# Heads of an attention block on one core: TensorE keeps the written order, both halves of an output-weight block run together behind a context, and one query moves from the start to the thirteenth head

## The chip, the cores and the metric

The kernel runs on one core of one Trainium2 chip. The core has a matrix engine (TensorE, "PE" in the profile, with its weight loads listed apart as "PEld"), a vector engine (VectorE, DVE), a scalar engine (ScalarE, ACT), a general engine (GpSimd, POOL) and a sync engine (SP) that here only issues DMAs. Each engine takes its own instructions strictly in the order in which they stand in its queue; an instruction whose operands or buffers are not ready makes everything behind it in that queue wait. The metric is the device time of one execution in microseconds (us), the median of several runs.

## The reference

Two transformer layers on `x` of shape (4, 512, 1024) in float32: four batches of 512 positions, 1024 wide.

```python
x = x + L0_attn(layernorm(x))   # attention over the batch axis, at each position of the width
x = x + L0_ffn(layernorm(x))    # 1024 -> 1024, and 2 of 8 low-rank experts per token
x = x + L1_attn(layernorm(x))   # below
x = x + L1_ffn(layernorm(x))    # 1024 -> 1024, and 8 low-rank experts weighted per batch
```

The change lies wholly in the third line, whose attention has 32 heads of width 128 (64 without and 64 with rotary position) and a shared latent of 64 for keys and values:

```python
q = rmsnorm(x @ wq_a.T) @ wq_b.T              # 1024 -> 256 -> 32 heads x (64 + 64)
ckv, k_pe = split(x @ wkv_a.T)                # 64 + 64, the same for all heads
kv = rmsnorm(ckv) @ wkv_b.T                   # 64 -> 32 heads x (64 key + 128 value)
q_pe, k_pe = rope(q_pe), rope(k_pe)
scores = einsum('bqhd,bkhd->bhqk', q, k) * scale     # causal mask, softmax
out = einsum('bhqk,bkhd->bqhd', softmax(scores), v)  # 512 x (32 x 128)
return out @ wo.T                                    # 4096 -> 1024
```

## The kernel before

Everything is one program, `block_kernel`. Products need close to float32 accuracy, so most operands are split into a rounded high part (type fp32r, names ending in `h`) and the remainder (`l`), and a product is three matmuls: `matmul3` (L148) does low x high, high x low, high x high in one PSUM bank.

The stages in order of time: layer 0 and the query, key and value projections of layer 1 (to 421.7 us), the *heads* (421.7 to 1488.3 us), and the last feed-forward. The change touches the heads alone.

**Units.** The 32 heads are four groups of eight (`NG`, `HG`); for each group come the four batches, and in each batch the eight heads: `units` is a list of 128 triples (g, b, i). One iteration of the loop over `u` works on several units at once, at different stages:

- `split_query(u + 1)` (L737): DVE makes the rounded copy `qh` (L741) and POOL the remainder `ql` (L742) of the next unit's query.
- `scores(u)`: four row tiles of 512, 384, 256 and 128 columns, one after another in a pool `pss` of two PSUM banks. The first three are `matmul3`, the last is one float32 matmul (L913). Each is followed by a DVE instruction that adds the causal mask and takes the minimum (L919) and by ACT's exponential (L922).
- `turn(u - 1)`: ten transposes of the previous unit's probabilities (L943) in three lots into a pool `pst` of two banks; the lots are copied to `pT` by ACT, ACT and DVE (L945).
- `context(u - 3)` on odd `u`, for two units at a time: eight matmuls 64 columns wide into `psv` (L959), and a DVE multiplication by the divisors (L962). The divisors go through a DRAM round trip on SP (`r_d`, `rb`).
- `query(u + 3)` (six matmuls into the single bank `psq`) and `rotate_query(u + 3)`: ACT copies it to `qf` (L729), DVE makes two half products from the bank (`wA`, L731 and L732), POOL multiplies and adds (L733, L734). Unit 2's query is issued in iteration 0, unit 3's likewise, and so on, three units ahead.
- a *filler*, a generator that is advanced by `per[0]`, `per[1]` and `per[2]` steps at three places of the iteration: behind the 384-column scores and the context, behind the 128-column scores and two lots of transposes, and behind the query.

**Two kinds of filler.** `project(g, b)` multiplies a finished batch's context by the group's output weights, in the seven-product form of Strassen and Winograd, twice (`j` = 0 and 2): products b11, t1, t2, b22, t3, b21, t4, each of two halves (so a filler step is half a product: "t40" is the first half of t4), accumulate in two banks `poa` and `pob`. After a product DVE adds the bank into a tile `xs` (L1036) that was fetched from DRAM and goes back there. The left operands `cxh` and `cxl` are made by ACT (L993) and POOL (L994). `prepare_output(g)` makes the group's output weights (value weights times `wo`): `block(n, half, at)` issues two matmuls 64 columns wide (L1069) into `poa` or `pob` from a room (`slotC`) that `fetch_output` fills by DMA (L1047, L1049); four blocks of two halves a group. ACT keeps a copy of a bank in one of six pieces of a room `raw` (`kept`, L1078) or makes a high part (`high`, L1083); the low parts and the differences between pieces (`low`, `less`) go to POOL when both operands are in `raw` (L1089, L1096), and to DVE when one is a bank (L1092, L1099). The names of the weights' tiles are those of the products: `b110h` is the high part of the first b11 tile, `t31h` that of the second t3 tile. For group 0 these steps run in the iterations u = 3 to 10, beside no projection; for groups 1 to 3 in four iterations at a time (u = 39 to 42 and so on), where the first batch of a group ends.

`prepare_query` (L677) makes a half group's query weights in the bank `pob`, from DRAM by `fetch_query`, in the iterations (b, i) = (3, 3) and (0, 0).

**What sets the order.** In the heads the framework's scheduler decides each engine's order from the written program, its own estimates and priorities, and `tc.issue_after(...)`, which holds an instruction behind a named one. On PE it moves work considerably: transposes, halves of a query and halves of products are found elsewhere than written. The last feed-forward already has `tc.manual_schedule(...)`, which makes the named engines take their instructions in the order of the program text.

## Time and profile before

| | us |
|---|---|
| median of 3 runs (lowest to highest) | 1746.12 (1744.06 to 1748.56) |
| the profiled execution | 1748.5 |
| its span, first to last instruction | 1746.3 |

The granted clock of TensorE is 0.997 of full speed over the span. Three stages of the span:

| stage | length, us | PE busy | DVE busy | ACT busy | POOL busy |
|---|---|---|---|---|---|
| before the heads, 0 to 421.67 | 421.67 | 401.39 | 316.29 | 170.06 | 127.64 |
| heads, 421.67 to 1488.30 | 1066.63 | 1056.85 | 802.24 | 631.01 | 651.43 |
| behind the heads, to 1746 | 257.70 | 246.40 | 187.10 | 102.43 | 146.21 |

How to read it. "Busy" is the time in which an instruction of the engine ran; an engine that waits for an operand is not busy. The span leaves out 2.2 us of the profiled execution's time, around the first and last instruction. A row of a timeline has the start in us, the duration, the engine, the line and the operation, the tile written and the tiles read, the shape, and in square brackets the idle time ahead of it and what ended that. A row of windows has the stretch, its length, the busy time and number of instructions of PE, PEld, DVE, ACT and POOL, the granted clock, the share of time in which the DMA engines were busy and the GB/s they moved.

### The profile page before, as it was taken

The page shows a single profiled execution, that of the slowest core. Times are in us where ns is not written, and L with a number is a line of the kernel's source. Part 1 is how long each engine was busy: PE and PEld are TensorE (multiplying, and loading weights), DVE is VectorE, ACT ScalarE, POOL GpSimd, SP SyncE. Part 2 cuts the span into 40 slices and gives each one's busy share as a digit, 9 for nine tenths or more (in the row PEclk, how much of TensorE's full clock was granted, in tenths as well). Part 3 has the DMA queues.
Part 4 walks back from the last instruction along what each step waited for, and adds up shares of the span by engine and source line. Part 5 has one row for each costly group of instructions (what it writes and reads, how often), then busy time and mean ns, then how long its engine had stood idle before and what let it go on. Part 6 is the DMA issues. An engine that isn't in the chain of part 4 may idle for free.

```text
span 1746.3 us, 31729 instructions
## 1 busy us (share of the span) xinstructions
PE 1704.6 (98%) x10536; PEld 1432.1 (82%) x10536; DVE 1305.6 (75%) x3494; ACT 903.5 (52%) x2316; POOL 925.3 (53%) x926
## 2 busy tenths in 40 slices
PE   7999999999999999999999999999999999999999
PEld 6899999998767777767787767778777877789998
DVE  7977885676877777787777677777778777687675
ACT  7422331365765565475555476555466555453332
POOL 0553541202666565666666656666556664675454
PEclk9999999999999999999999999999999999999999
DMA  5313543245324234353333353242344333853431
GB/s 194 134 42 116 183 161 114 89 137 166 103 92 140 97 108 148 98 175 113 113 126 105 113 183 116 97 148 94 130 159 156 108 101 121 308 199 123 138 110 68
DMA packets 131940, 228.17 MB, mean 131 GB/s; under 512 B 22272, under 2 KB 58752, under 8 KB 128448
## 3 DMA queue, kind: packets, MB, share of 16 engines
q1 hardware_dynamic: 131776, 226.13, 38.7%
q8 instruction: 84, 1.38, 0.3%
q14 instruction: 80, 0.66, 0.1%
HBM read 156.60 MB, written 71.83 MB: 131 GB/s over the span
## 4 chain that ended last, share of the span: by engine, by line
PE 85%; DVE 7%; DMA 3%; ACT 2%; POOL 2%; issue 2%; SPq 0%; DVEq 0%; ACTq 0%; POOLq 0%
PE psv L959 8%; PE pst L943 8%; PE pss L150 4%; PE po L150 4%; PE po L152 4%; PE po L151 4%; PE pss L151 4%; PE pss L152 4%; PE pob L150 3%; PE psq L150 3%; PE poa L150 3%; PE psq L151 3%; PE psq L152 3%; PE pob L152 3%; PE pob L151 3%; PE acc L150 3%
## 5 line engine op out<-in xcount | busy, mean ns | idle before, releaser
L922 ACT ACTIVATE p<-p,mn 128x512 f32<-128x512 f32 (+3 forms) x512 | 284.6, 558 | 218.6 <-DVE mn L919 214.3
L919 DVE CUSTOM_DVE_ANT_0 p<-pss,causal 128x512 f32<-128x512 f32 (+3 forms) x512 | 232.4, 486 | 29.1 <-PE pss L152 21.9
L733 POOL TENSOR_TENSOR qf<-qf,ropeT 64x512 f32<-64x512 f32 x128 | 164.5, 1285 | 167.1 <-ACT qf L729 165.1
L943 PE MATMUL pst<-ident,p 128*128 128x128 f32 x1280 | 186.1, 273 | 3.7 <-ACT pT L945 3.7
L734 POOL TENSOR_TENSOR qf<-qf,wA 64x512 f32<-64x512 f32 x128 | 164.5, 1285 | 31.2 <-DVE wA L732 24.8
L943 PEld LDWEIGHTS pst<-ident,p 128*128 128x128 f32 x1280 | 153.0, 141 | 31.1 <-ACT pT L945 8.2
L742 POOL TENSOR_TENSOR ql<-qf,qh 128x384 fp32r<-128x384 f32 x128 | 131.1, 1024 | 63.9 <-DVE qh L741 47.6
L994 POOL TENSOR_TENSOR cxl<-s,cxh 128x256 fp32r<-128x256 f32 x128 | 96.8, 764 | 119.0 <-ACT cxh L993 65.1
L945 ACT COPY pT<-pst 128x512 f32<-128x512 f32 x256 | 142.4, 578 | 23.3 <-PE pst L943 21.3
L150 PE MATMUL pss<-kT,ql 128*128 128x512 f32 (+2 forms) x384 | 144.0, 375 | 0.8 <-DVE mn L919 0.4
L150 PE MATMUL po<-w_h,hTl 128*128 128x384 f32 (+1 forms) x384 | 133.1, 347 | 0.8 <-DVE x L433 0.8
L151 PE MATMUL pss<-kT,qh 128*128 128x512 f32 (+2 forms) x384 | 131.5, 342 | 0.0
L152 PE MATMUL pss<-kT,qh 128*128 128x512 f32 (+2 forms) x384 | 130.4, 340 | 0.0
L152 PE MATMUL po<-w_h,hTh 128*128 128x384 f32 (+1 forms) x384 | 130.1, 339 | 0.0
L151 PE MATMUL po<-w_l,hTh 128*128 128x384 f32 (+1 forms) x384 | 129.7, 338 | 0.0
L945 DVE COPY pT<-pst 128x256 f32<-128x256 f32 x128 | 54.3, 424 | 94.2 <-PE pst L943 93.1
L729 ACT COPY qf<-psq 128x512 f32<-128x512 f32 x126 | 74.0, 587 | 71.7 <-PE psq L152 71.7
L731 DVE TENSOR_TENSOR wA<-psq,ropeT 32x512 f32<-32x512 f32 x126 | 87.7, 696 | 22.5 <-ACT qf L729 19.5
L994 POOL TENSOR_TENSOR cxl<-cx,cxh 128x256 fp32r<-128x256 f32 x96 | 73.7, 769 | 55.6 <-ACT cxh L993 53.1
L922 ACT ACTIVATION_READ_ACCUMULATOR p<-p,mn 128x1 f32 x512 | 96.9, 189 | 0.0
L150 PEld LDWEIGHTS pss<-kT,ql 128*128 128x128 f32 x384 | 72.6, 189 | 21.9 <-DVE mn L919 4.3
L732 DVE TENSOR_TENSOR wA<-psq,ropeT 32x512 f32<-32x512 f32 x126 | 87.0, 691 | 1.7
(511 smaller groups left out, 4979.1 us busy)
## 6 DMA issues: line engine op xcount, KB each, us to landing
xs<-x_d SPq DMA_DIRECT2D x128, 256.0 KB
x_d<-xs SPq DMA_DIRECT2D x128, 256.0 KB
slotC<-in_woT_dram SPq DMA_DIRECT2D x32, 512.0 KB
rb<-r_d SPq DMA_DIRECT2D x128, 128.0 KB
w_t<-raw SPq DMA_DIRECT2D x32, 288.0 KB
x<-in_x_dram SPq DMA_DIRECT2D x16, 512.0 KB
x_d<-x SPq DMA_DIRECT2D x32, 256.0 KB
slotA<-q_d SPq DMA_DIRECT2D x8, 1024.0 KB
```

The costliest lines, as they stand in the source:

```text
L150: T.matmul(ps, lhsT=al, rhs=bh, start=start, stop=False, **kw)
L151: T.matmul(ps, lhsT=ah, rhs=bl, start=False, stop=False, **kw)
L152: T.matmul(ps, lhsT=ah, rhs=bh, start=False, stop=stop, **kw)
L733: G.tensor_tensor(f[mid], f[mid], ropeT[mid, 0, :], ALU.mult)
L734: G.tensor_tensor(f[mid], f[mid], t2[mid], ALU.add)
L742: G.tensor_tensor(l, f[:, P:S], f32(h), ALU.subtract)
L919: turn_of[0] = V.tensor_tensor_reduce(out=to, in0=ps[:, 0:n], in1=causal[:, S - n : S], scale=1.0, scalar=-NEG, op0=ALU.add, op1=ALU.min, ...
L922: A.activation(to, to, AF.Exp, bias=mn[:, i : i + 1], scale=-1.0, accum_out=rs[:, i : i + 1])
L943: T.transpose(ps[:, w : w + P], p[:, OF[i] + j * P : OF[i] + (j + 1) * P], ident)
L945: copy(pT[:, AT[js[0]] : AT[js[0]] + w], ps[:, 0:w])
L959: T.matmul(ps[n * KVR : (n + 1) * KVR, S - w : S], lhsT=k[:, j, :], rhs=pTs[u + n][:, AT[j] : AT[j] + w], start=(j == 0), stop=(j == TPB - 1))
L994: G.tensor_tensor(l, src, f32(h), ALU.subtract)
```

## The change

It has six parts, all in the heads:

1. `manual_schedule` for TensorE: its instructions of the heads stay in the order of the program text. The other engines are still ordered by the scheduler.
2. Queries come two units ahead instead of three up to u = 12 (`EXTRA`), and three ahead afterwards; iteration 12 issues two of them (units 14 and 15), so one query moves from the start to the thirteenth head. Up to u = 12 `split_query(u + 1)` stands behind the first advance of the filler.
3. A block of the output weights does both halves, in `poa` and `pob`, in one step, behind a context. Four of these steps a group replace eight; `per` for group 0 becomes (1, 1, 1), and for heads 4 to 7 of a group's first batch (2, 2, 2).
4. The differences and low parts of the output weights are taken in another order and with other pieces: more of them are between pieces of `raw`, which puts them on POOL, and there are fewer copies on ACT. Group 0 has an order of its own.
5. `less` looks only at its two operands to choose the engine, so a difference can be written from a bank into `raw`.
6. `prepare_query` moves from the iteration into `project`, ahead of each half (`j` = 0 and 2), into the bank whose turn it is; a list `fetched_q` holds what was fetched.

```diff
--- before.py
+++ after.py
@@ -849,6 +849,7 @@
         xsp = c2.enter_context(tc.tile_pool(name="c2_x", bufs=5, side="right"))
         pso = c2.enter_context(tc.tile_pool(name="c2_pso", bufs=1, space=PSUM, side="right"))
         heads = c2.enter_context(ExitStack())
+        heads.enter_context(tc.manual_schedule(engines={T.engine}))
         tp = heads.enter_context(tc.tile_pool(name="c2_t", bufs=3))
 
 
@@ -1014,6 +1015,9 @@
                             splitter(cxp, HG // 4, "cx"))
             parts = [next(outs), next(outs)]
             for j in range(0, TPB, 2):
+                if fetched_q:
+                    n, fetched = fetched_q.pop(0)
+                    wqs[n] = prepare_query(fetched, pso, "po" + "ab"[(1 + j // 2) % 2])
                 at, xs, banks = {}, {}, {}
                 for t, k in ((0, 0), (1, 1), (0, 1), (1, 0)):
                     at[t, k] = x_d[b * TPB + j + t][k]
@@ -1060,15 +1064,16 @@
             prs = [c + k for c in range(HG // 4) for k in (0, HG // 4)]
             po, tiles = {}, {}
 
-            def block(n, half, at):
+            def block(n):
                 nonlocal fetched
                 wo, wv = fetched
-                po[at] = pso.tile([P, 512], F32, name="po" + at)
                 with ExitStack() if g else tc.issue_after(scored[0].ins):
-                    for k in range(2):
-                        T.matmul(po[at][k * KVR : (k + 1) * KVR, :], lhsT=wv[:, k, :],
-                                 rhs=wo[k][:, half * 512 : half * 512 + 512], start=True, stop=True)
-                if half and n + 1 < len(prs):
+                    for half, at in enumerate("ab"):
+                        po[at] = pso.tile([P, 512], F32, name="po" + at)
+                        for k in range(2):
+                            T.matmul(po[at][k * KVR : (k + 1) * KVR, :], lhsT=wv[:, k, :],
+                                     rhs=wo[k][:, half * 512 : half * 512 + 512], start=True, stop=True)
+                if n + 1 < len(prs):
                     fetched = fetch_output(g, prs[n + 1])
 
             def src(at):
@@ -1092,89 +1097,66 @@
                     V.tensor_tensor(l, src(at), f32(h), ALU.subtract)
 
             def less(to, a0, a1):
-                if not {to, a0, a1} & set(po):
+                if not {a0, a1} & set(po):
                     G.tensor_tensor(src(to), src(a0), src(a1), ALU.subtract)
                     return
                 with tc.issue_after(turn_of[0].ins):
                     V.tensor_tensor(src(to), src(a0), src(a1), ALU.subtract)
 
             def steps():
-                block(0, 0, "a")
-                yield
-                kept(0, "a")
-                high("b11", "a")
-                block(0, 1, "b")
-                yield
-                low("b11", "a")
-                kept(1, "b")
-                yield
-                less("b", "b", 0)
-                block(1, 0, "a")
...
+                for n in (0, 2):
+                    block(n)
+                    yield
+                    kept(1, "b")
+                    yield
+                    high("b11", "a")
+                    less(4, 1, "a")
+                    yield
+                    low("b11", "a")
+                    yield
+                    high("t1", 4)
+                    yield
+                    low("t1", 4)
+                    yield
+                    block(n + 1)
+                    yield
+                    if g == 0:
+                        kept(3, "b")
+                        less(5, "b", 4)
+                        high("b21", "a")
+                        yield
+                        kept(2, "a")
+                        high("b22", 3)
+                        low("b21", "a")
+                        yield
+                        high("t2", 5)
+                        low("b22", 3)
+                        less(3, 3, 1)
+                        low("t2", 5)
+                        yield
+                        high("t3", 3)
+                        less(2, 2, 5)
+                        low("t3", 3)
+                        yield
+                    else:
+                        less(5, "b", 4)
+                        high("b22", "b")
+                        yield
+                        low("b22", "b")
+                        less(2, "a", 5)
+                        high("b21", "a")
+                        yield
+                        less(3, "b", 1)
+                        low("b21", "a")
+                        high("t2", 5)
+                        yield
+                        low("t2", 5)
+                        high("t3", 3)
+                        low("t3", 3)
+                        yield
+                    high("t4", 2)
+                    low("t4", 2)
+                    yield
 
             return steps()
 
@@ -1211,7 +1193,9 @@
                     nc.sync.dma_start(out=tiles[t][:, k * 512 : (k + 1) * 512], in_=x_d[2 * q + t][k])
 
         filler = None
+        fetched_q = []
         cx = None
+        EXTRA = 12
         for u in range(NU + 3):
 
 
@@ -1219,12 +1203,12 @@
             g, b = divmod(B, NB)
             if i == 0 and B > 0:
                 filler = project(*divmod(B - 1, NB))
-            per = ((4, 1, 0) if i % 2 else (1, 1, 0)) if b else (2 + (i < HG // 2 + 2), 2, 2) if i >= HG // 2 else (3, 3, 1)
+            per = ((4, 1, 0) if i % 2 else (1, 1, 0)) if b else (2, 2, 2) if i >= HG // 2 else (3, 3, 1)
             if B == 0:
-                per = (0, 1, 2)
+                per = (1, 1, 1)
             if b == 0 and i == (HG // 2 if g else 0) and g < NG:
                 filler = prepare_output(g, wo_raw)
-            if u + 1 < NU:
+            if EXTRA < u < NU - 1:
                 split_query(u + 1)
             sc = scores(u) if u < NU else iter(())
             tn = turn(u - 1) if 0 < u <= NU else iter(())
@@ -1234,10 +1218,11 @@
             advance(sc)
             advance(cx)
             advance(filler, per[0])
+            if u <= EXTRA:
+                split_query(u + 1)
 
             if u == 0:
                 query(2, psq, "psq")
-                rotate_query(2)
             advance(sc)
             advance(sc)
             advance(tn)
@@ -1245,15 +1230,18 @@
             advance(filler, per[1])
             if u < NU:
                 g, b, i = units[u]
-                if (b, i) == (NB - 1, 3) and g + 1 < NG:
-                    wqs[2 * g + 2] = prepare_query(wq_raw, pso, "pob")
-                if (b, i) == (0, 0) and g > 0:
-                    wqs[2 * g + 1] = prepare_query(wq_raw, pso, "pob")
-            if u + 3 < NU:
+            if 0 < u <= EXTRA:
+                query(u + 2, psq, "psq")
+            if u <= EXTRA:
+                rotate_query(u + 2)
+            if EXTRA < u < NU - 3:
                 query(u + 3, psq, "psq")
                 rotate_query(u + 3)
             advance(filler, per[2])
             advance(tn)
+            if u == EXTRA:
+                query(u + 3, psq, "psq")
+                rotate_query(u + 3)
             if u < NU:
                 g, b, i = units[u]
                 if i == 2 and u + HG < NU:
@@ -1262,7 +1250,8 @@
                 if b == 0 and i == 0:
                     wo_raw = fetch_output(g, 0)
                 if (b, i) in ((NB - 1, 0), (NB - 1, 4)) and g + 1 < NG:
-                    wq_raw = fetch_query(2 * g + 2 + i // 4)
+                    n = 2 * g + 2 + i // 4
+                    fetched_q.append((n, fetch_query(n)))
                 if (g, b) == (NG - 1, NB - 1) and i == 1:
                     late = raw()
                     hs = {0: [late[:, (t + 1) * D : (t + 2) * D] for t in range(2)]}
```

More of the change, by code (lines that the diff above doesn't have):

```diff
@@ L1101, in steps @@
             def steps():
-                block(0, 0, "a")
-                yield
-                kept(0, "a")
-                high("b11", "a")
-                block(0, 1, "b")
-                yield
-                low("b11", "a")
-                kept(1, "b")
-                yield
-                less("b", "b", 0)
-                block(1, 0, "a")
-                yield
-                high("t1", "b")
-                kept(0, "b")
-                kept(2, "a")
-                high("b21", "a")
@@ L1118, in steps @@
-                yield
-                low("t1", "b")
-                low("b21", "a")
-                block(1, 1, "b")
-                yield
-                high("b22", "b")
-                kept(3, "b")
-                yield
-                low("b22", 3)
-                less("b", "b", 0)
-                block(2, 0, "a")
-                yield
-                high("t2", "b")
-                kept(5, "a")
-                less(3, 3, 1)
-                yield
-                low("t2", "b")
@@ L1135, in steps @@
-                less("b", 2, "b")
-                high("b11", "a")
-                yield
-                high("t4", "b")
-                high("t3", 3)
-                low("b11", "a")
-                yield
-                low("t4", "b")
-                low("t3", 3)
-                block(2, 1, "a")
-                yield
-                kept(1, "a")
-                yield
-                less("a", "a", 5)
-                block(3, 0, "b")
-                yield
-                high("t1", "a")
@@ L1152, in steps @@
-                kept(5, "a")
-                kept(2, "b")
-                high("b21", "b")
-                yield
-                low("t1", "a")
-                low("b21", "b")
-                block(3, 1, "a")
-                yield
-                high("b22", "a")
-                kept(3, "a")
-                yield
-                low("b22", 3)
-                less("a", "a", 5)
-                yield
-                high("t2", "a")
-                less(3, 3, 1)
-                yield
@@ L1169, in steps @@
-                low("t2", "a")
-                less("a", 2, "a")
-                high("t3", 3)
-                yield
-                high("t4", "a")
-                low("t3", 3)
-                yield
-                low("t4", "a")
-                yield
+                for n in (0, 2):
[51 more added lines that the diff above has]
+                    yield
```

## Prediction

> **What bounds the kernel now.** I read the page's engine table first, then the stages by window, then the order of instructions on TensorE (PE) against its helpers.

> ```profile
> PE 1704.6 (98%) x10536; PEld 1432.1 (82%) x10536; DVE 1305.6 (75%) x3494; ACT 903.5 (52%) x2316; POOL 925.3 (53%) x926
> ```

> PE is the bound. Only its waits and the form of its order can change the time: the change adds and removes no matmul. The heads run from 421.7 to 1488 us. By windows (length, then busy us of PE, PEld, DVE, ACT, POOL, then the granted clock):

> ```profile
> 426.00:430.00 4.00, 1.32 (x6) 0.85 (x5) 2.30 (x5) 0.75 (x2) 3.24 (x4) 1.00 0.96 281
> 430.00:436.00 6.00, 5.62 (x18) 4.19 (x18) 3.22 (x12) 3.52 (x11) 2.61 (x3) 0.50 0.32 104
> 442.00:515.00 73.00, 70.75 (x402) 50.09 (x401) 58.42 (x162) 52.75 (x142) 47.63 (x42) 1.00 0.34 116
> 515.00:676.00 161.00, 161.00 (x911) 126.66 (x910) 119.55 (x325) 91.62 (x256) 100.35 (x98) 1.00 0.34 112
> 742.00:800.00 58.00, 57.20 (x317) 39.19 (x314) 46.99 (x124) 42.00 (x108) 37.74 (x35) 1.00 0.47 152
> ```

> The first two are the start (2.7 us idle, then half clock), 442 to 515 is heads 3 to 13, 515 to 676 heads with projection and not one idle PE moment, 742 to 800 the output weights of group 1. So nearly every microsecond by which PE waits anew is lost. An even-numbered u with projection, from the timeline:

> ```profile
> 622.33 0.39 PE L152 MATMUL psq<-slotB,wqh 128*128 128x512 f32 x1
> ...
> 622.76 0.59 ACT L729 COPY qf<-psq 128x512 f32<-128x512 f32 x1 [0.57 <-PE psq L152]
> ...
> 623.42 0.70 DVE L731 TENSOR_TENSOR wA<-psq,ropeT 32x512 f32<-32x512 f32 x1
> ...
> 624.85 0.69 DVE L919 CUSTOM_DVE_ANT_0 p<-pss,causal 128x512 f32<-128x512 f32 x1
> ...
> 625.46 0.55 DVE L919 CUSTOM_DVE_ANT_0 p<-pss,causal 128x384 f32<-128x384 f32 x1
> ...
> 625.85 0.40 PE L152 MATMUL poa<-b211h,cxh 128*128 128x512 f32 x1
> ...
> 625.94 0.68 DVE L1036 TENSOR_TENSOR xs<-xs,pob 128x512 f32<-128x512 f32 x1
> ...
> 626.08 0.28 PE L150 MATMUL pss<-kT,ql 128*128 128x256 f32 x1
> ...
> 626.77 0.47 PE L150 MATMUL pob<-t40h,cxl 128*128 128x512 f32 x1
> ```

> The query's last matmul gives way at 622.56; call such a moment Q. Behind it stand, in DVE's order, the rotation (L731, L732) from Q+0.86, the masks of 512 and 384 columns from Q+2.29 and Q+2.90, and the sum L1036, which ends at 626.62. Product t40 accumulates in the bank that the sum reads and starts 0.15 us after its end. PE fills the time with the 256-column and 128-column scores.

> **The change, step by step.** The built order of the changed kernel gives what stands where. Sums go against the profiled execution: 1748.5 us with a span of 1746.3, 2.4 above the median of the runs, 1746.1.

> *1. t40 in the projection.* PE's order as written puts t40's first half directly behind b21, ahead of the 256-column scores; DVE's order there is unchanged. PE is ready at 626.08 and may start at 626.77: 0.69 us of waiting, and the scores queued behind have no cover left to give. In before the same place loses 0.10 (626.55 to 626.77 instead of 0.11), so 0.58 net. The timeline shows the pattern 19 times (530.08, 562.33, 594.54, 626.77, 659.91, five and five again, four in the last group). Of the other five, three (690, 961, 1232) escape because the query was put later; as written it is not: 0.69 each. The last two have no query before them. 19 x 0.58 + 3 x 0.69 = **+13.1**. Ends: 0, if the sum gets done earlier, and 22 x 0.69 = 15.2.

> *2. Even heads without projection (u = 2, 4, 8).* In before the scheduler put eight transposes and half a query between the 384- and the 256-column scores (440.64 to 442.48). As written nothing is between: PE arrives at Q + 0.22 (two transposes) + 0.70 + 0.53 = Q+1.45. The 256-column scores need the buffer that the 512-column mask frees at Q+2.98, plus 0.15: Q+3.13, and the 128-column ones the 384 mask, Q+3.45 plus 0.15. Waiting 1.65 + 0.14 = 1.8 each: **+5.4**. Odd heads have context (2.3) and block in that place and wait for nothing. Ends 0 and 6.

> *3. u = 6 and 10 (seventh and eleventh head).* In before a chain of GpSimd (POOL) work of the output weights stops PE once:

> ```profile
> 491.61 1.28 POOL L1096 TENSOR_TENSOR raw<-raw 128x512 f32<-128x512 f32 x1
> ...
> 492.92 0.62 ACT L1083 CAST t31h<-raw 128x512 fp32r<-128x512 f32 x1 [2.48 <-POOL raw L1096]
> ...
> 493.45 0.72 ACT L922 ACTIVATE p<-p,mn 128x512 f32<-128x512 f32 x1
> ...
> 495.64 1.05 ACT L945 COPY pT<-pst 128x512 f32<-128x512 f32 x2
> ...
> 496.26 0.44 PE L943 MATMUL pst<-ident,p 128*128 128x128 f32 x2 [2.25 <-ACT pT L945]
> ```

> ScalarE (ACT) waits for POOL, its exponentials and copies of transposes queue behind, and PE's third group of transposes lacks a buffer. The change puts ten subtractions into POOL's queue for group 0 plus four, where six were, and queries come two heads ahead, not three. For u = 6 POOL's order is: b220l, two subtractions, first rotation of query 7, t20l, t30l, second rotation, t40l, ql. From Q of u = 4: the second block ends at 1.45 + 2.4 + 1.9 = 5.75; four ACT copies at 0.5 to 0.6 each bring b220h at 7.7; seven POOL pieces (five subtractions, two rotations) at 1.35 bring 17.2. DVE then makes qh (0.3), which stands ahead of the 256-column mask in its queue, and the mask (0.4); ACT two exponentials (0.9) and a copy (0.5): PE's transposes go on at 19.5. Without waits PE is there after an odd head (1.45 + 2.4 + 1.9 + 0.58 + 0.87 + 1.39 = 8.6) and an even one's 4.3, at 12.9. 6.6 lost. u = 10 has the same pieces in another order; I take the same. 2 x 6.6 - 2.25 (the old stop) = **+11.0**. Ends 2.25 and 8 for each head.

> *4. The additional query (u = 12).* In before query 3 runs at 429.05, inside idle time at the start, 6 x 0.23 = 1.4 us. The start's chain (masks from 430.58, behind a DMA) stays, so the early slot is not made use of, and 1.4 is paid between full heads. Its bank is single and query 14 is just before it: like the 2.68 us gap at 426.4, PE waits for the rotation, Q+2.4 plus 0.15 against Q+0.22: 2.3. **+3.7**, ends 0 and 4.1.

> *5. Blocks.* Blocks and contexts are 64 columns wide.

> ```profile
> 485.43 0.39 PE L152 MATMUL psq<-slotB,wqh 128*128 128x512 f32 x1
> 485.75 1.08 PE L1069 MATMUL poa<-slotC 128*64 128x512 f32 x4
> 486.76 0.44 PE L943 MATMUL pst<-ident,p 128*128 128x128 f32 x2
> ```

> Entry costs 0.32 here where a product gives way after 0.23, and the exit 0.10 more: 0.19 a round trip. By the order, 87 runs of 64-wide instructions become 70: 17 x 0.19 = **-3.2**. The waits of the output-weight stretches (0.49 and 0.31 three times, 0.61 at 1293) go: **-3.0**. In groups 1 to 3 two blocks are now one head apart: 4.3 us of PE work lie between, while a fetch takes from 745.25 to about 749.7 in the packets, with wake-up 4.7. 0.4 x 6 = **+2.4**, ends 0 and 7 (behind the 1 MB load of the next batch).

> *6. SP and the rest.* Four fetches a group as before; query weights come as many heads ahead. The ACT copies saved (0.5 us each) lie beside PE: nothing.

> *7. The clock.* 2.7 us idle, after gaps of 0.56 and 0.48, was followed by 6 us at 0.50, which lost 3; 2.25 us idle at 494 kept 1.00. The new gaps, about 2 and 4 us, stand amid work; I take 0, end +6. [...]

> Sum: 13.1 + 5.4 + 11.0 + 3.7 - 3.2 - 3.0 + 2.4 = **+29.4**: 1777.9 against the profiled execution, 1775.5, say **1776**, on the median's scale.

> **Rivals.** *A: the GpSimd chain costs only what it cost before* (2.25 a head, so -8.7): 1767. For it: ACT and POOL are each under 75% busy there. Against: POOL takes turns strictly in the rows above.
> *B: no wait at t40* (-13.1): 1762. It needs DVE's sum 0.7 us earlier; but the 19 rows agree to 0.02 us.
> *C: two clock drops as at 430* (+6): 1782.
> *D, the other side: the order as written has no hazards*, because DVE gets to the masks early. From the 39th to the 44th head before needs 50.4 us for 48.0 of PE work, three times 2.4; the first twelve take 82.2 for 77.2. Saved 7.2 + 5.0: 1734. It decides from a mask start at Q+1.3 or sooner on and needs POOL clear of item 3; the rows have Q+2.29.
> *E: the order hardly differs where it counts*: 1746. For it: heads with projection are the same but for t40.

> **Numbers.** Forecast 0.45, A 0.13, B 0.12, C 0.10, D 0.14, E 0.06. 0.3% is 5.2 us, about what can be told from no change: faster 0.14, same 0.06, slower 0.80. The range 1757 to 1790 holds all but D and E: its low end is B with A's half, its high end the forecast with C, 8 us heads and slow fetches.

> **What would show it.** Right: PE idle before pob/poa of t40 by about 0.6 at some 22 places; PE idle over 5 us in each of the seventh and eleventh heads, ended by ACT's pT; 1.7 us before the 256-column scores in heads 3, 5 and 9; 2.3 before the second query of head 13. Wrong: 161 us windows in the middle still at 100% PE, or head 13 reached by 516 us instead of about 530.

## The result and the profile after

The changed kernel takes 1786.1 us (median of 4 runs, 1784.3 to 1789.3; before, on the same chip, 1745.8), 1.0228 times the time before, interval 1.0212 to 1.0243: slower by some 40 us. The forecast was 1776 in a range of 1757 to 1790. The profiled execution took 1785.8 with a span of 1783.9. Its engine table has for TensorE (PE):

```profile
PE 1700.8 (95%) x10536; PEld 1431.3 (80%) x10536; DVE 1291.1 (72%) x3480; ACT 892.9 (50%) x2288; POOL 945.2 (53%) x940
```

As many matmuls as before, busy for 1700.8 us where it was 1704.6, in a span 38 us longer: the whole loss is waiting and clock. Three stretches by window, first of the kernel after (the 1st to 15th head's last scores, to the 31st, to the 51st), then the same heads before; the columns are as in the prediction:

```profile
429.50:551.31 121.81, 102.83 (x537) 73.49 (x536) 72.59 (x206) 67.98 (x185) 74.03 (x65) 0.91 0.24 78
551.31:683.52 132.21, 130.05 (x738) 101.80 (x737) 96.51 (x261) 74.39 (x208) 81.01 (x79) 1.00 0.35 111
683.52:860.10 176.58, 169.70 (x953) 129.00 (x951) 128.40 (x340) 99.58 (x273) 109.74 (x105) 1.00 0.41 135
```

```profile
432.14:529.75 97.61, 95.07 (x527) 69.54 (x527) 75.83 (x212) 68.30 (x187) 63.44 (x57) 0.98 0.28 94
529.75:659.59 129.84, 129.84 (x739) 102.34 (x737) 96.76 (x262) 74.26 (x209) 81.10 (x80) 1.00 0.35 114
659.59:833.09 173.50, 172.61 (x953) 129.47 (x951) 130.99 (x344) 103.08 (x282) 105.93 (x103) 1.00 0.41 136
```

The first fourteen heads lose 24.2 us, the sixteen beside projection 2.4, the twenty around an output-weight stretch 3.1. The other stretches repeat the last two kinds: over all heads +40, to which the medians' 40.3 fit. (The changed profile reaches the heads 2.5 us earlier, with TensorE's order there unchanged; that belongs to the two executions.)

The places that the prediction named, in timelines of the kernel after. t40, in every fourth head beside projection, 22 times:

```profile
582.08 0.39 PE L152 MATMUL poa<-b211h,cxh 128*128 128x512 f32 x1
582.18 0.68 DVE L1040 TENSOR_TENSOR xs<-xs,pob 128x512 f32<-128x512 f32 x1
583.01 0.47 PE L150 MATMUL pob<-t40h,cxl 128*128 128x512 f32 x1 [0.54 <-DVE xs L1040]
```

The sum L1040 ends at 582.86 and t40 starts 0.15 later, as before, but nothing is left to fill the 0.54. Where no projection runs, the heads of even u from 2 to 10, by count the third, fifth, seventh, ninth and eleventh ("even heads" below means even u), have this:

```profile
452.90 0.69 DVE L732 TENSOR_TENSOR wA<-psq,ropeT 32x512 f32<-32x512 f32 x1
453.62 0.69 DVE L920 CUSTOM_DVE_ANT_0 p<-pss,causal 128x512 f32<-128x512 f32 x1
454.37 0.39 PE L150 MATMUL pss<-kT,ql 128*128 128x256 f32 x1 [1.74 <-DVE mn L920]
```

The 512-column mask stands behind the rotation, and the 256-column scores wait for the buffer that it frees. In the kernel before, transposes and half a query filled the place, and nothing waited; this is its third head:

```profile
440.64 1.04 PE L943 MATMUL pst<-ident,p 128*128 128x128 f32 x8
441.72 0.47 PE L150 MATMUL psq<-slotA,wql 128*128 128x512 f32 x1
...
442.48 0.28 PE L150 MATMUL pss<-kT,ql 128*128 128x256 f32 x1
```

The seventh head of the changed kernel goes on like this:

```profile
468.62 1.28 POOL L733 TENSOR_TENSOR qf<-qf,ropeT 64x512 f32<-64x512 f32 x1
...
469.98 1.28 POOL L1094 TENSOR_TENSOR t20l<-raw,t20h 128x512 fp32r<-128x512 f32 x1
...
471.22 1.29 POOL L1094 TENSOR_TENSOR t30l<-raw,t30h 128x512 fp32r<-128x512 f32 x1
...
472.58 1.26 POOL L734 TENSOR_TENSOR qf<-qf,wA 64x512 f32<-64x512 f32 x1
473.88 0.36 DVE L741 CAST qh<-qf 128x384 fp32r<-128x384 f32 x1 [4.21 <-POOL qf L734]
...
474.15 0.42 DVE L920 CUSTOM_DVE_ANT_0 p<-pss,causal 128x256 f32<-128x256 f32 x1
...
475.51 1.05 ACT L946 COPY pT<-pst 128x512 f32<-128x512 f32 x2
...
476.12 0.69 PE L944 MATMUL pst<-ident,p 128*128 128x128 f32 x2 [3.65 <-ACT pT L946]
```

Read it from the end: TensorE waits 3.65 us for a copy on ScalarE, that for an exponential, that for the 256-column mask, that (in VectorE's queue) for the rounded copy `qh`, that for the second half of the rotation on GpSimd, and between the two halves of the rotation GpSimd makes two low parts of output weights. (That the mask stood in the queue: the last matmul of its scores started at 469.58 and took 0.28, and VectorE began the mask at 474.15, right behind `qh`.) In the thirteenth head the second query waits for `wA`, the rotation of the first (first row). In groups 1 to 3 the second and fourth block of a stretch wait for their fetch:

```profile
535.02 0.47 PE L150 MATMUL psq<-slotB,wql 128*128 128x512 f32 x1 [2.02 <-DVE wA L732]
...
773.39 1.08 PE L1074 MATMUL poa<-slotC 128*64 128x512 f32 x4 [1.29 <-DMA slotC<-in_wv_dram]
...
790.43 1.08 PE L1074 MATMUL poa<-slotC 128*64 128x512 f32 x4 [2.06 <-DMA slotC<-in_wv_dram]
```

And the clock (the third figure from the end), in windows of 3.41 us laid out from the start of half clock at 474.52:

```profile
471.11:474.52 3.41, 1.37 (x6) 0.75 (x5) 0.64 (x4) 0.00 (x0) 3.25 (x4) 1.00 0.14 50
474.52:477.93 3.41, 1.80 (x6) 1.52 (x7) 1.32 (x6) 2.43 (x7) 2.54 (x3) 0.50 0.00 0
477.93:481.35 3.42, 3.42 (x10) 1.38 (x10) 2.30 (x7) 1.42 (x4) 2.51 (x3) 0.50 0.00 0
488.18:491.59 3.41, 1.69 (x13) 1.30 (x11) 3.17 (x7) 1.15 (x4) 3.25 (x3) 1.00 0.65 238
491.59:495.00 3.41, 3.41 (x13) 2.92 (x12) 0.91 (x5) 2.39 (x8) 1.23 (x2) 0.50 0.23 82
```

Behind the stop of the seventh head TensorE runs at half clock for 6.83 us, and behind a stall of only 1.72 us in the ninth for 3.41. Two more such stretches start at 515.48 and 535.96. None of the four is in the profile before; the half clock at the start of the heads, 6.83 us (from 426.73, before from 430.00), is in both.

### The profile page after: what moved, and what is told of

Same layout as the page of the kernel before. It is cut to its first block, busy times and chain, and to the rows that moved or that the text cites. A ratio compares the mean times of both kernels' runs of the same rounds, so it can differ in the third digit from the quotient of the medians.

```text
span 1783.9 us, 31654 instructions
## 1 busy us (share of the span) xinstructions
PE 1700.8 (95%) x10536; PEld 1431.3 (80%) x10536; DVE 1291.1 (72%) x3480; ACT 892.9 (50%) x2288; POOL 945.2 (53%) x940
## 4 chain that ended last, share of the span: by engine, by line
PE 79%; DVE 10%; DMA 4%; POOL 3%; ACT 2%; issue 2%; SPq 0%; POOLq 0%; DVEq 0%; ACTq 0%
PE psv L960 8%; PE pst L944 6%; PE po L150 4%; PE po L152 4%; PE po L151 4%; PE pss L150 3%; PE psq L151 3%; PE pss L151 3%; PE psq L150 3%; PE psq L152 3%; PE pob L150 3%; PE pss L152 3%; PE poa L150 3%; PE acc L150 2%; PE acc L152 2%; PE acc L151 2%
## 5 line engine op out<-in xcount | busy, mean ns | idle before, releaser
L733 POOL TENSOR_TENSOR qf<-qf,ropeT 64x512 f32<-64x512 f32 x128 | 164.6, 1286 | 178.1 <-ACT qf L729 176.4
L734 POOL TENSOR_TENSOR qf<-qf,wA 64x512 f32<-64x512 f32 x128 | 164.7, 1286 | 20.9 <-DVE wA L732 14.1
L150 PE MATMUL pss<-kT,ql 128*128 128x512 f32 (+2 forms) x384 | 145.1, 378 | 16.3 <-DVE mn L920 16.0
L150 PE MATMUL po<-w_h,hTl 128*128 128x384 f32 (+1 forms) x384 | 132.9, 346 | 0.0
L152 PE MATMUL pss<-kT,qh 128*128 128x512 f32 (+2 forms) x384 | 131.4, 342 | 0.0
L152 PE MATMUL po<-w_h,hTh 128*128 128x384 f32 (+1 forms) x384 | 130.1, 339 | 0.0
L729 ACT COPY qf<-psq 128x512 f32<-128x512 f32 x126 | 74.3, 589 | 76.6 <-PE psq L152 75.6
L150 PEld LDWEIGHTS pss<-kT,ql 128*128 128x128 f32 x384 | 73.3, 191 | 44.6 <-DVE mn L920 19.5
L731 DVE TENSOR_TENSOR wA<-psq,ropeT 32x512 f32<-32x512 f32 x126 | 87.6, 695 | 25.1 <-ACT qf L729 22.3
L732 DVE TENSOR_TENSOR wA<-psq,ropeT 32x512 f32<-32x512 f32 x126 | 87.0, 691 | 1.7
```

Of the source, the lines that this page charges most:

```text
L150: T.matmul(ps, lhsT=al, rhs=bh, start=start, stop=False, **kw)
L152: T.matmul(ps, lhsT=ah, rhs=bh, start=False, stop=stop, **kw)
L733: G.tensor_tensor(f[mid], f[mid], ropeT[mid, 0, :], ALU.mult)
L734: G.tensor_tensor(f[mid], f[mid], t2[mid], ALU.add)
```

## The experiments

Ratios are to the kernel before on the same chip, with 95% intervals; "against the changed kernel" is the difference to its 1.0228, times 1746 us.

| run | ratio (interval) | against the changed kernel |
|---|---|---|
| t40 behind the scores | 1.0134 (1.0119 to 1.0150) | -16 |
| queries three ahead | 1.0211 (1.0184 to 1.0237) | -3 |
| transposes first | 1.0216 (1.0197 to 1.0235) | -2 |
| no written order | 1.0071 (1.0056 to 1.0086) | -27 |
| block late | 1.0229 (1.0214 to 1.0244) | 0 |
| group 0 in the others' order | 1.0193 (1.0176 to 1.0210) | -6 |
| low parts on VectorE | 1.0142 (1.0125 to 1.0159) | -15 |
| queries two ahead all through | 1.0274 (1.0259 to 1.0290) | +8 |
| two parts | 1.0060 (1.0044 to 1.0075) | -29 |
| all | 1.0061 (1.0048 to 1.0075) | -29 |
| written order from head 14 | 1.0017 (1.0008 to 1.0026) | -37 |
| written order beside projection only | 0.9988 (0.9979 to 0.9996) | -42 |

**t40 behind the scores.**

```diff
-per = ((4, 1, 0) if i % 2 else (1, 1, 0)) if b else ...
+per = ((4 - i % 4 // 3, 1 + i % 4 // 3, 0) if i % 2 else (1, 1, 0)) if b else ...
```

> The changed kernel with one filler step moved: in every second even head with projection the first half of t4 is advanced behind the 128-column scores and two lots of transposes, not ahead of the 256-column scores. Theory 'separate waits' (each part's loss is its own and local): the 22 gaps of 0.53 to 0.55 us ahead of t40 go, 22 x 0.59 = -12.9 us against the changed kernel (1786.1): about 1773. Rival 'written order' (the losses belong to the fixed order as a whole; a wait taken away at one place comes back at the next): under half of it, 1780 or more, with new gaps ahead of the 256-column scores or of t41.

The 22 gaps are gone and none came in their place; the profile has no gap over 0.25 us between the 14th head and the first output-weight stretch. Four heads beside projection take 32.05 us, where they took 32.83 in the changed kernel and 32.24 before. That is 0.78 for each t40, 17 in all: more than the 0.59 that was expected, because without that wait the written order takes 0.19 less than the scheduler's for the four heads.

**Queries three ahead.** Edit: `EXTRA = 12` becomes `EXTRA = 0`.

> The changed kernel with EXTRA = 0: queries come three heads ahead from the start, the additional query stands in the first head again, and the query's split stands ahead of the scores. Theory 'lead' (two heads ahead leave too little time for the GpSimd chain): the stops of 3.65 and 4.25 us in heads 7 and 11, the 2.02 in head 13, the 1.4 us of the additional query and the half clock behind the three (about 2.6 + 1.7 + 1.7 us lost) go, and at most the 2.25 us of the kernel before comes back: 1769 to 1772. Rival 'GpSimd's load' (the added subtractions make POOL late whatever the lead): stops of over 3 us stay in heads 7 and 11, and only the additional query with its wait and clock goes, about -5: 1781. The waits of 1.4 to 1.7 us ahead of the 256-column scores in even heads stay under both.

The theory of the lead falls. The head that made two queries is down to 8.34 us from 13.52, but the stops are still there, 4.11 and 3.15 us, with GpSimd's queue as before: L733, `t20l`, `t30l`, L734. The additional head of lead was used up on VectorE: in its queue the scheduler has pulled the split forward by a head, so that `qh` again takes the query that was rotated last, again stands ahead of a mask, and waits for the same second half:

```profile
478.58 1.26 POOL L734 TENSOR_TENSOR qf<-qf,wA 64x512 f32<-64x512 f32 x1
479.87 0.36 DVE L741 CAST qh<-qf 128x384 fp32r<-128x384 f32 x1 [4.63 <-POOL qf L734]
...
481.49 0.44 PE L944 MATMUL pst<-ident,p 128*128 128x128 f32 x2 [4.11 <-ACT pT L946]
```

What more lead would bring with the cast kept behind the mask, no run tested. The additional query, back in the first head, costs there: 6.50 us from the first to the second head's last scores for 4.06.

**Transposes first.**

```diff
+            early = u % 2 == 0 and u <= 10
+            if early:
+                advance(tn, 2)
             advance(sc)
             advance(sc)
-            advance(tn)
-            advance(tn)
+            if not early:
+                advance(tn, 2)
```

> The changed kernel with the first two lots of transposes ahead of the 256-column scores, in even heads up to u = 10. Theory 'masks stand behind the rotation' : eight transposes, 0.79 us from start to start, cover as much of the 1.43, 1.74 and 1.72 us in heads 3, 5 and 9, -2.4 us, and -1.7 more if the half clock behind the third goes with it: 1782 to 1784. Heads 7 and 11 end with POOL as before. Rival 'written order': the transposes are missing behind the 128-column scores, and the time is lost there: 1786.

-2, where -2 to -4 was expected; the interval alone doesn't tell it from nothing, but the rows say more. The waits of 1.43 and 1.74 in heads 3 and 5 are 0.58 and 0.86. In the seventh head the transposes are now done early, and TensorE stops one step later at the other end of the same chain, at `ql`:

```profile
472.27 1.26 POOL L734 TENSOR_TENSOR qf<-qf,wA 64x512 f32<-64x512 f32 x1
...
475.02 0.99 POOL L742 TENSOR_TENSOR ql<-qf,qh 128x384 fp32r<-128x384 f32 x1
...
476.06 0.79 PE L150 MATMUL pss<-kT,ql 128*128 128x512 f32 x1 [4.72 <-POOL ql L742]
```

In this run, too, the stop ends with GpSimd's queue.

**No written order.** Edit: the line with `manual_schedule` is left out.

> The changed kernel without the written order on TensorE: the scheduler orders it again, all else stays. Theory 'separate waits': t40 (-12.9) and the waits of the even heads (-4.9, and -1.7 of clock) go, the stops from POOL, the additional query and the waits of the blocks for their fetch stay: about 1766. Rival 'written order': all comes back, 1748 or less.

-27, between the two theories. No gap is left at t40 and the even heads wait 0.4; but the stops of the seventh and eleventh heads are 4.23 us each, and the first fourteen intervals from last scores to last scores take 110.5 us where they took 97.6 before. Of the loss, what goes with the fixed order is about two thirds. The rest lies in the first fourteen heads: the stops behind GpSimd's work on the output weights, and the additional query (the thirteenth head takes 11.10 us, before 8.38); the run doesn't separate these.

**Group 0 in the others' order, and low parts on VectorE.**

```diff
-                    if g == 0:
+                    if g < 0:
                         kept(3, "b")
```

> The changed kernel with group 0's output weights made in the order of groups 1 to 3, which takes eight subtractions on GpSimd where the changed kernel takes fourteen (the kernel before: six). Theory 'GpSimd's load': the stops of 3.65 and 4.25 us in heads 7 and 11 fall to at most the 2.25 of the kernel before in one of them, and the half clock behind them (2.6 + 1.7 us lost) goes with them: -9 to -12, 1774 to 1777. Rival 'place of the split' (the rounded copy qh stands ahead of the 256-column mask in VectorE's queue and waits for the rotation, however little else GpSimd has to do): stops of over 3 us stay, 1784 or more.

```diff
-                if at not in po:
+                if g and at not in po:
                     G.tensor_tensor(l, src(at), f32(h), ALU.subtract)
                     return
```

> The changed kernel with group 0's ten low parts from raw on VectorE; four differences are left on GpSimd. Theory 'GpSimd's load': the stops in heads 7 and 11 go with their half clock, -10 to -13, 1773 to 1776. Rival 'VectorE takes its place' (ten subtractions of about 0.7 us stand in VectorE's queue ahead of masks and copies and wait there for ScalarE's high parts): the stops stay in another form, 1783 or more.

The first gave -6, half of what was expected: there too two low parts (`t20l`, `t40l`) stand between the halves of the rotation, and a stop of 1.88 us is left in the seventh head. The second gave -15. With the low parts gone from GpSimd's queue the halves are neighbours:

```profile
466.92 1.28 POOL L733 TENSOR_TENSOR qf<-qf,ropeT 64x512 f32<-64x512 f32 x1 [0.86 <-ACT qf L729]
468.36 1.27 POOL L734 TENSOR_TENSOR qf<-qf,wA 64x512 f32<-64x512 f32 x1 [0.16 <-DVE wA L732]
...
473.34 0.50 PE L150 MATMUL pss<-kT,ql 128*128 128x512 f32 x1 [0.90 <-POOL ql L742]
```

0.90 us is left of the stop, and none in the eleventh head. Of the four new stretches of half clock two are left, behind the wait of 1.71 ahead of the eleventh head's 256-column scores and in the thirteenth head (a new one follows at 1053.73). The theory of GpSimd's load holds. The first of the two runs shows that the place of the load counts too: of only eight subtractions two still stood between the halves.

**Queries two ahead all through.**

```diff
-        EXTRA = 12
+        EXTRA = NU
...
-            if u == EXTRA:
-                query(u + 3, psq, "psq")
-                rotate_query(u + 3)
```

(The conditions of the other queries are bounded by `NU` instead of `EXTRA`.)

> The changed kernel with queries two heads ahead all through, with no additional query in head 13. Theory 'load, not lead' (three heads ahead left the stops of heads 7 and 11 where they were, so the lead was not what was short): only the additional query's 1.4 us, its wait of 2.02 and the half clock behind it (1.7) change, -5.1: 1781. Rival 'lead beside projection' (with GpSimd busy at 62% there, a query split one head ahead comes late for the 512-column scores): 0.3 us or more in each of a hundred heads, over 1805.

Slower, and by a third way. The thirteenth head takes 8.51 us for 13.52, so the additional query's 5.0 is shown. Beside projection the shorter lead costs 0.13 us in four heads (32.96 for 32.83), not 0.3 in each. But in the output-weight stretches the chain of the seventh head now appears, in each group:

```profile
779.09 1.27 POOL L1094 TENSOR_TENSOR t30l<-raw,t30h 128x512 fp32r<-128x512 f32 x1
780.33 1.27 POOL L1094 TENSOR_TENSOR t40l<-raw,t40h 128x512 fp32r<-128x512 f32 x1
...
781.68 1.28 POOL L734 TENSOR_TENSOR qf<-qf,wA 64x512 f32<-64x512 f32 x1
782.99 0.36 DVE L741 CAST qh<-qf 128x384 fp32r<-128x384 f32 x1 [3.25 <-POOL qf L734]
...
786.50 0.44 PE L944 MATMUL pst<-ident,p 128*128 128x128 f32 x2 [2.87 <-ACT pT L946]
```

There three ahead is what keeps it away. So the lead is not without worth; in the first heads it does not help.

**Block late.**

```diff
-... else (2, 2, 2) if i >= HG // 2 else (3, 3, 1)
+... else ((0, 3, 3) if g and i % 2 else (2, 2, 2)) if i >= HG // 2 else (3, 3, 1)
```

> The changed kernel with, in groups 1 to 3, the filler advanced (0, 3, 3) in place of (2, 2, 2) in the second and fourth head of an output-weight stretch, so that the second and fourth block stand behind the 128-column scores and two lots of transposes, some 2.5 us of TensorE work later. Theory 'fetch': the waits of the blocks for their DMA (1.29 and 2.06, 1.60 and 2.18, 1.44 and 2.24 us, together 10.8) go, six round trips of 0.19 for 64-wide runs of their own come, +1.1: -9.7 against the changed kernel, 1776. Rival 'one room' (blocks go at the pace of the one room they are fetched into; the next block then waits instead): the third and the following waits appear, -3 or less: 1783.

No wait for a fetch is left in the first stretch, and the time is the same. The block was the cover of the masks:

```profile
774.17 0.69 DVE L920 CUSTOM_DVE_ANT_0 p<-pss,causal 128x512 f32<-128x512 f32 x1
...
774.92 0.39 PE L150 MATMUL pss<-kT,ql 128*128 128x256 f32 x1 [1.74 <-DVE mn L920]
```

Both theories fall in the form given: no later block waits, but another wait stood behind the first, 1.74 and 1.45 us a stretch. That is less idle time than the 10.8 and 5.5 of the changed kernel's stretches, 9.6 for 16.3; but two of the waits of 1.74 were followed by half clock, 3.41 us each from 776.01 and 1052.49. What made up the rest is open.

**Two parts, and all.** The first joins t40 behind the scores and the low parts on VectorE. The second adds, in even heads up to u = 12 and in the stretches, this ahead of the filler's first advance (and leaves them out at their old places):

```diff
+            if early:
+                n = u + 2 if u <= EXTRA else u + 3
+                advance(tn, 2)
+                if u <= EXTRA:
+                    split_query(u + 1)
+                query(n, psq, "psq")
+                rotate_query(n)
             advance(filler, per[0])
```

> The changed kernel with t40 behind the scores and group 0's low parts on VectorE, nothing else. Theory 'separate waits': the two gains add up, -16 and -14: 1756. Rival 'the cover moves': with one gone the other costs more, 1762 or more.

> The changed kernel with t40 behind the scores, group 0's low parts on VectorE, and in the even heads up to u = 12 and of the output-weight stretches two lots of transposes and the whole query (0.8 and 1.4 us of TensorE work) ahead of the block and the 256-column scores. Theory 'separate waits': the two parts bring what they brought alone (-16 and -14); the waits ahead of the 256-column scores in heads 3 to 11, 9.0 in the run with low parts on VectorE with the stop of 0.90, one half-clock window (1.7), head 13's wait of 2.02 with its window (1.7), together -14.4; the fetches (-10.8): 1786 - 55 = 1731, faster than the kernel before (1746). Rival 'the cover moves' (as in the run with the later blocks, what is put ahead of one wait is missing at the next): the last two items bring a third or less, 1748 or more.

The two parts add up within the intervals: -16 and -15 alone, -29 together. The rest brought nothing, as the rival had it. It took away waits of 1.43 to 1.74 us, but `qh` and the low parts then stand ahead of work that is due, and stops of 2.27 and 2.30 us at `ql` come back in heads 7 and 11; in the stretches the fetches still cost 0.4 to 1.0 us, and new waits of 0.3 to 0.8 came.

**Written order from head 14, and beside projection only.** Both have the first 13 heads of the kernel before (its steps, blocks and queries) and t40 behind the scores.

```diff
+            if (u >= 13 and b > 0) != ordered:
+                ordered = not ordered
+                if ordered:
+                    region.enter_context(tc.manual_schedule(engines={T.engine}))
+                else:
+                    region.close()
```

(This is the second; in the first the order begins at u = 13 and holds to the end of the heads.)

> The first 13 heads as in the kernel before (the scheduler orders TensorE, queries three ahead, blocks in single halves, six subtractions on GpSimd); from the 14th head on the changed kernel with the written order and t40 behind the scores. Theory 'separate waits': the start takes what it took before, and the rest what it took in the run of the two parts, 948.3 us from the 15th head's last scores to the last head's where the kernel before takes 949.3 (four heads beside projection 32.05 for 32.24, given back by fetches in the output-weight stretches): 1745, no difference that can be told. Rival 'written order': fixing the order costs by itself, 1752 or more.

> As the run before it, but the written order holds only in the heads beside projection of a group's second to fourth batch; in the output-weight stretches the scheduler orders TensorE, with the changed kernel's steps. Theory 'separate waits': 22 times four heads at 32.05 for 32.24 bring -4, the stretches take 123.9 as in the run without the written order (before: 124.5): 1742. Rival: where the written order begins and ends the scheduler loses it again, 1746 or more.

The first: 1750.4 us, 11 runs from 1745.8 to 1752.1, and 1.0008 at the least: 0.2% slower where no difference was expected. The execution with the profile took 1746.7, so what the others lost isn't in it and stays open. The granted clock can be only a part of it: it was 0.999 in that execution and 0.994 to 0.997 in the other ten, but 0.997 in both the fastest and the slowest. The second is the one version that beats both kernels: 1744.7 us for 1747.1 beside it, 0.1%, small, but its interval leaves out 1; half of the 4 us expected. Four heads beside projection take 32.06 us, as with t40 moved.

## Why the prediction was right, and where its terms were off

The kernel is slower by the mechanisms named, at the places named: 22 gaps at t40; over 5 us of idle in heads 7 and 11, of which 3.65 and 4.25 were ended by `pT` and 1.46 and 1.74 by the mask; about 1.7 ahead of the 256-column scores in heads 3, 5 and 9; 2.02 ahead of the second query; head 13 at 529.3 where 530 was said. The sum was 10 us short: +29.4 for +40. That head 13 came so near to 530 is partly luck: up to there half clock added some 6 us that were not in the sum (an estimate, half of the 12.0 us in which TensorE was busy at it), while the even heads and the chain cost 2.6 less than predicted and this execution reached the heads 2.5 us earlier.

| term | predicted | measured |
|---|---|---|
| 1, t40 | +13.1 | +13.0: 22 x 0.59 from four heads' 32.83 and 32.24 |
| 2, even heads | +5.4 | +4.9: 1.43 + 1.74 + 1.72 |
| 3, heads 7 and 11 | +11.0 | +8.9: 5.11 + 5.99 - 2.25 |
| 4, additional query | +3.7 | +3.4: 2.02 + 1.4 (with some 1.7 of clock, the 5.0 of the run with two ahead) |
| 5, blocks | -3.8 | +3.6 over the three stretches, t40 taken out |
| 7, clock | 0 | +7.7 |

These are 41.5; about -1.4 is spread over the first heads and the ends.

**Term 1** was right in place and number (22), and its nearness to 0.1 is luck: the wait was 0.53 to 0.55 where 0.69 was said, taking it away brought 0.78, and 0.19, which the prediction did not have, is gained elsewhere in the same four heads. Rival B, no wait there, falls.

**Term 3** was right in its chain, link by link. Of its two causes only one is shown: in the run with three ahead "queries come two heads ahead, not three" made no difference there (the cast came a head earlier with them); the run with low parts on VectorE shows that GpSimd's additional pieces did. The term was 2.1 too large: 5.11 and 5.99 for 6.6 each. Rival A, that the chain costs only what it did, falls.

**Term 5** is the first step that failed, in its size: "a fetch takes from 745.25 to about 749.7", so 0.4 us of waiting. In the changed kernel it is 5.7 us from the issue at 767.66 to the block at 773.39, and 6.6 from 783.87 to 790.43; the waits are 1.29 and 2.06, 1.60 and 2.18, 1.44 and 2.24, together 10.8 for the 2.4 predicted. (The profile puts the last of the six down to a mask; its block starts 6.7 us after its fetch was issued, like the fourth.) "The waits of the output-weight stretches go" was wrong too: two others came at their end, 1.10 and 0.85 us in the first, 5.5 in all three, for 3.0 that went. Against this stands -9.7 that I have only as the remainder; fewer 64-wide runs are part of it (in heads 31 to 51 sixteen runs with 32.1 us, from the start of each to the next matmul, became twelve with 30.2, some -2 a stretch), so that -3.2 was too small; the other part is open. The run with the late blocks shows that another wait stood behind the fetch's, so that the 10.8 would not have come back with it.

**Term 7** is the second: "about 2 and 4 us, stand amid work; I take 0, end +6". Stalls of 3.65, 4.25 and 2.02 us in the first heads, and one of 1.72, were followed by half clock: 6.83 + 3 x 3.41 us, in which TensorE was busy for about 15.5; half of that, 7.7, is my estimate of the loss. (At 536 matmuls of 512 columns start 0.43 us apart at half clock, just before it 0.23; by these starts it would be 7.1.) Rival C, 1782, was nearest to the time, with two drops for the four that came. The time lies in the range, near its top, though these two, some 7 us each, were missing from the sum: the range had room for them.

**Terms 2 and 4** were right in size (the 1.4 was not measured by itself). That a wait's length is not what its removal brings is shown for term 2 by the run with all parts.

## What to carry to other kernels

When an engine's order is fixed by hand, look at every place where the scheduler had put other work between a producer and its consumer: each such place may become a wait, whose length can be estimated from the time that the old trace shows filled. Where a wait is removed, read what is next in line there before counting its length as gain; of the edits here that took a wait away, two brought its length and three hardly anything, because of the next one. Low-priority work that is put into an in-order queue between two halves of urgent work can cost its length on the path (two low parts of 1.28 us; a stop of 3.65 became 0.90 without them), and more lead did not cure it here, where another queue tied the consumer to the same moment.

## What the runs showed of the hardware

| idle in the window | after: windows, followed by half clock | before |
|---|---|---|
| 2.02 to 2.82 us | 4, all 4 | 1 (2.46), 1 |
| 1.72 to 1.88 us | 6, 1 | 1 (1.72), 0 |
| 1.25 to 1.69 us | 8, 0 | 3, 0 |

None of these windows was idle throughout. In the run with all parts one with 1.48 us, at 503.88, was followed by half clock too. In the middle row the idle time alone does not tell which: in the changed kernel 1.72 us at 488.18 was followed by half clock, and these were not, the eleventh head's equal stall among them:

```profile
505.24:508.65 3.41, 1.67 (x15) 1.60 (x14) 2.12 (x6) 0.83 (x3) 3.25 (x4) 1.00 0.53 158
508.65:512.06 3.41, 1.55 (x8) 0.96 (x6) 0.00 (x0) 1.68 (x5) 3.33 (x3) 1.00 0.00 0
```

What else decides is open. Before, the 2.25 us at 494 were divided between two windows, 0.84 and 1.41 idle, and no half clock followed:

```profile
491.44:494.85 3.41, 2.57 (x16) 1.91 (x14) 1.95 (x7) 1.93 (x6) 2.60 (x3) 1.00 0.83 319
494.85:498.27 3.42, 2.01 (x14) 1.89 (x15) 2.34 (x7) 3.16 (x11) 2.20 (x4) 1.00 0.12 40
498.27:501.68 3.41, 3.41 (x17) 2.12 (x16) 2.80 (x11) 3.27 (x10) 2.62 (x3) 1.00 0.53 166
```

The same stop of 2.24 us in the run with written order from head 14 lay within one window, and half clock followed:

```profile
490.91:494.32 3.41, 1.17 (x6) 0.67 (x6) 0.94 (x6) 3.41 (x12) 2.00 (x3) 1.00 0.57 231
494.32:497.74 3.42, 3.42 (x14) 2.88 (x13) 2.96 (x7) 1.87 (x5) 3.19 (x4) 0.50 0.30 81
```

**Subtractions on VectorE that met GpSimd took longer.** In the run with all parts a subtraction of two SBUF tiles on VectorE took 0.69 us where it started ahead of an instruction of GpSimd (`t10l`), and 1.76 where it started 0.05 behind one (`t20l`):

```profile
458.58 0.69 DVE L1097 TENSOR_TENSOR t10l<-raw,t10h 128x512 fp32r<-128x512 f32 x1
458.70 1.72 POOL L734 TENSOR_TENSOR qf<-qf,wA 64x512 f32<-64x512 f32 x1 [0.22 <-DVE wA L732]
...
470.91 1.26 POOL L1101 TENSOR_TENSOR raw<-raw 128x512 f32<-128x512 f32 x1 [0.69 <-DVE b220l L1097]
470.96 1.76 DVE L1097 TENSOR_TENSOR t20l<-raw,t20h 128x512 fp32r<-128x512 f32 x1
```

In these two pairs the longer one is the one that started second: GpSimd's 1.72 for the 1.28 that L734 takes on average in the kernel before, VectorE's 1.76 for 0.69. The subtraction `b210l`, with one operand in PSUM, took 0.68 (at 464.43), with GpSimd at work on L1101 from 464.59 to 465.89. So a low part that was moved from GpSimd to VectorE, `t20l`, still met GpSimd.
